# Layer 1's x_w product in halves of a chunk on two column tiles, its step sizes over all rows, and its output as 128 and twice 64 channels

## The chip, the core and the metric

The kernel runs on one core of one Trainium2 chip. The time is the device time of one execution in microseconds (us). The core has TensorE (PE, the matrix engine; PEld is its loading of weights), VectorE (DVE), ScalarE (ACT), GpSimd (POOL) and SyncE (SP, which here only issues DMAs). They run their own instruction streams and wait for each other by semaphores. All data are float32.

## The reference

Four layers work on an image batch of 4 x 64 x 64 positions and 192 channels, each as x + layer(group norm of x). The change is in layer 1, where four selective scans (forward and backward along rows, forward and backward along columns) run on 384 inner channels with 16 states each. For one direction, with `xs` a set of lines of 64 positions:

```python
xz = jnp.einsum('nlc,dc->nld', xs, in_w)
u, z = jnp.split(xz, 2, axis=-1)
uc = silu(conv(u, cw) + cb)                  # 4 taps along the line
x_dbl = jnp.einsum('nld,ed->nle', uc, xw)    # 12 + 16 + 16 rows
dt, Bp, Cp = jnp.split(x_dbl, [DT_RANK, DT_RANK + DS], axis=-1)
delta = jax.nn.softplus(jnp.einsum('nlr,dr->nld', dt, dtw) + dtb)
# step: h = exp(delta * A) * h + delta * uc * B;  y = sum over the states of h * C
y = (y + uc * Dv) * silu(z)
out = jnp.einsum('nld,cd->nlc', y, ow)
```

The results of the four directions are joined and multiplied with `fc_w`. Layers 0 and 3 are two-dimensional selective scans with the same inner loop and layer 2 is a Toeplitz mixing; the change leaves their arithmetic alone.

## The kernel before

Channels lie on the partitions. Layer 1 (`mamba`, L678) first multiplies `fc_w` into the four output matrices, and then makes 128 jobs: 4 directions x 4 images x 8 chunks of T = 512 positions. Directions 1 and 3 are backward and add to what the direction before them has put in DRAM (`done`, written as `m_out`).

**One job.** `mamba_job` (L752) loads the chunk (`xn`, L771), multiplies with `in_w` in three blocks of 128 channels (`input_of`, in_ps, L777), convolves on DVE (L794) and applies silu on ACT. `prepare` (L189) makes the small products: `project` (L196) is x_w's product, 44 x 512 (xd_ps, L211); ACT copies it to `xd` and sends its B and C rows to DRAM (L221); `turn_b` (L232) transposes B; `step_size` (L246) makes the step sizes of one block of 128 channels out of the 12 rows 32 to 43 of `xd` (dt_ps, L261); `finish` applies softplus and forms dtu = delta * u; `turn` transposes dtu. `gate` multiplies with the other half of `in_w` (z_ps). `out` (L817) multiplies with the output matrix, in two pieces of 96 channels (o_ps, L821), and stores to `m_out` (L829); in a backward direction `earlier` (L814) has loaded the values to add.

`project` and `step_size` have a second form, used where `halves` is true, which in this kernel is layer 0 alone: the chunk is split in two halves of 256 positions, whose products stand on partitions 0 to 63 and 64 to 127.

**The units.** The scan itself goes in 24 units a job, each 64 channels with two pairs of states, 128 x 1024 elements. For a unit, `feed` (L340) has TensorE make b = delta * u * B in PSUM by 8 matmuls (L360) and ACT make dA = exp(delta * A) (L383); `scan` has DVE run the recurrence (L393) and POOL multiply by C (hc, L405); `collect` has TensorE sum over the states (y, L423). In 6 of the 24 units (those of one state pair) b is made by POOL (`spread`, bs, L337) in place of TensorE; in a job they are units 2, 5, 10, 13, 18 and 21, counted from 0. b's PSUM pool has two buffers, so the b of a unit waits for the scan two units before.

**The loads.** `fetch` (L295) brings the operands from DRAM to SBUF by SP: C (c) and, for POOL's b, B (bc), each row broadcast over 64 partitions (L325), and the channel rows delta (both) and dtu, each twice, by a source with a leading dimension of 2 (L312). The pools have 4 buffers for c, 4 for both and 2 each for bc and dtu, so a load waits in SP's queue until the unit that used the buffer is done.

**The order.** `run_jobs` (L104) walks all units and puts each job's steps at a number of units before or after the job's first unit: chunk load at -48, `input_of` at -45, -32 and -29, `project` -24, `turn_b` -22, `step_size` -20, -18 and -17, `out` at 32 and 35. The steps of one job so fall among the units of the two jobs before it. A scheduler then settles the order on each engine from estimated times; the engines keep to it.

Of the kernel before, what the change touches and what calls it, by code (L numbers as in the profile page):

```python
# [7 lines left out]
F32 = mybir.dt.float32  # L8
AF = mybir.ActivationFunctionType
# [4 lines left out]
B, HW, L = 4, 64, 4096  # L14
C = 192
PC, KC = 96, 2
N = 16
R = 12
E = R + 2 * N
T = 512  # L20
# [16 lines left out]
class Kernel:  # L37
# [151 lines left out]
    def prepare(self, job, pools):  # L189

        nc = self.nc
        prep, mm = pools["prep"], pools["mm"]
        P, NT, DI, w = job["P"], job["NT"], job["DI"], job["w"]
        halves = job["carry"] is not None and NT == 3

        def project():  # L196
            u = job["u"]
            if halves:

                ps = mm.tile([128, 256], F32, name="xd_ps", tag="mm")  # L200
                for t in range(NT):
                    for h in range(2):
                        nc.tensor.matmul(
                            ps[h * 64 : (h + 1) * 64, :], w["xw"][:, t, :], u[:, t, h * 256 : (h + 1) * 256],
                            start=t == 0, stop=t == NT - 1,
                        )
                xd = job["xd"] = prep.tile([128, 256], F32, name="xd", bufs=1)
            else:
                ps = mm.tile([E, T], F32, name="xd_ps", tag="mm")
                for t in range(NT):  # L210
                    nc.tensor.matmul(ps, w["xw"][:, t, 0:E], u[:, t], start=t == 0, stop=t == NT - 1)  # L211
                xd = job["xd"] = prep.tile([E, T], F32, name="xd", bufs=1)
            nc.scalar.copy(xd, ps)
            job["bc"] = self.bcd.tile([2 * N, T], F32, name="bc_dram")
            if job["carry"] is None:

                by_half = job["bc"].rearrange("(a n) l -> a (n l)", n=2).rearrange(
                    "a (h n l) -> h a n l", h=2, n=2
                )
                for h in range(2):  # L220
                    nc.scalar.dma_start(by_half[h], xd[0 : 2 * N, h * 256 : (h + 1) * 256])  # L221
            elif halves:
                by_half = job["bc"].rearrange("a (h l) -> h a l", h=2)
                for h in range(2):
                    nc.scalar.dma_start(by_half[h], xd[h * 64 : h * 64 + 2 * N, :])
            else:
                nc.scalar.dma_start(job["bc"], xd[0 : 2 * N, :])
            job["delta"] = prep.tile([P, NT, T], F32, name="delta", bufs=1)
            job["dtu"] = prep.tile([P, NT, T], F32, name="dtu", bufs=1)
            job["dtuT"] = prep.tile([128, NB, DI], F32, name="dtuT",)  # L230

        def turn_b():  # L232
            bt = job["bt"] = prep.tile([128, NB, N], F32, name="bt")
            if halves:
                ps = mm.tile([128, 2, 128], F32, name="b_ps", tag="mm")
                for k in range(2):
                    nc.tensor.transpose(ps[:, k, :], job["xd"][:, k * 128 : (k + 1) * 128], self.ident)
                of = ps.rearrange("p k (h e) -> p k h e", h=2)[:, :, :, 0:N]
                nc.scalar.copy(bt.rearrange("p (h k) n -> p k h n", h=2), of)
                return  # L240
            ps = mm.tile([128, NB, N], F32, name="b_ps", tag="mm")
            for k in range(NB):
                nc.tensor.transpose(ps[:, k, :], job["xd"][0:N, k * 128 : (k + 1) * 128], self.ident[:N, :N])
            nc.scalar.copy(bt, ps)

        def step_size(t):  # L246
            if halves:

# [12 lines left out]
            nc.tensor.matmul(  # L261
                dp, w["dtw"][2 * N : E, t * P : (t + 1) * P], job["xd"][2 * N : E, :], start=True, stop=True
            )
            nc.scalar.activation(job["delta"][:, t, :], dp, AF.Identity, bias=w["dtb"][:, t : t + 1])

        def finish():
            delta = job["delta"]
            nc.scalar.activation(delta, delta, AF.Softplus)  # L268
            (nc.gpsimd if job["carry"] is None else nc.vector).tensor_mul(job["dtu"], delta, job["u"])  # L269
            if job["carry"] is not None:  # L270
                return
            job["deltas"] = self.bcd.tile([DI, T], F32, name="delta_dram")
            nc.scalar.dma_start(job["deltas"].rearrange("(t p) l -> p t l", p=P), delta)

        def turn(t):
            ps = mm.tile([128, NB, P], F32, name="dtu_ps", tag="mm")
            for k in range(NB):
                nc.tensor.transpose(  # L278
                    ps[:, k, :], job["dtu"][:, t, k * 128 : (k + 1) * 128], self.ident[:P, :P]
                )  # L280
            nc.scalar.copy(job["dtuT"][:, :, t * P : (t + 1) * P], ps)  # L281

        def store_dtu():
            job["dtus"] = self.bcd.tile([DI, T], F32, name="dtu_dram")
# [393 lines left out]
    def mamba(self, x_in):  # L678
# [3 lines left out]
        DI = P * NT  # L682
        pre = "L1_"
        by_row, by_col = self.image_tiles("m_row"), self.image_tiles("m_col")
        done = [self.image_tiles(f"m_out{i}_") for i in range(2)]

        both_w = [self.dram.tile([P, NT, C], F32, name=f"m_both_w{i}") for i in range(4)]
        bufs = dict(c=4, bc=2, diag=4, both=4, dtu2=2)
# [63 lines left out]
    def mamba_job(self, pw, pin, mm, i, begin, rev, w, x, done, both_w, c, fixed, zero):  # L752
# [6 lines left out]
        job = {}  # L759

        def weights():
            for name in ("in_w", "conv_w", "conv_b", "A", "D", "x_w", "dt_b"):
                w[name] = self.load(pw, name, ins[pre + name][i])
            w["dtw"] = pw.tile([E, DI], F32, name="dt_w")
            nc.sync.dma_start(w["dtw"][2 * N : E, :], ins[pre + "dt_w"][i])
            w["out_w"] = self.load(pw, "out_w", both_w)
            w["xw"], w["dtb"] = w["x_w"], w["dt_b"]
            self.neg_exp(w["A"])

        def load():  # L770
            job["xn"] = self.load(pin, "xn", x[:, :, s])  # L771
# [37 lines left out]
        def gated(t):  # L809
            u, z = job["u"][:, t, :], job["z"][:, t, :]  # L810
            nc.vector.scalar_tensor_tensor(u, u, w["D"][:, t : t + 1], job["y"][t], ALU.mult, ALU.add)
            nc.gpsimd.tensor_mul(z, z, u)

        def earlier(m):  # L814
            job.setdefault("o", {})[m] = self.load(pin, "o", done[:, m, s])

        def out(m):  # L817
            o = job["o"][m] if rev else pin.tile([PC, T], F32, name="o")
            ps = mm.tile([PC, T], F32, name="o_ps", tag="mm")
            for t in range(NT):  # L820
                nc.tensor.matmul(  # L821
                    ps, w["out_w"][:, t, m * PC : (m + 1) * PC], job["z"][:, t, :],
                    start=t == 0, stop=t == NT - 1,
                )
            if rev:
                nc.vector.tensor_add(o, ps, o)
            else:
                nc.scalar.copy(o, ps)
            nc.sync.dma_start(done[:, m, s], o)  # L829

        when = dict(project=-24, turn_b=-22, step_size=(-20, -18, -17), finish=-15, turn=(-10, -7, -3), store=-11)
        each = lambda f, ats: [(at, lambda t=t: f(t)) for t, at in enumerate(ats)]
        steps = [(-50, weights)] if begin else []
        steps += [(-48, load)] + each(input_of, (-45, -32, -29)) + each(gate, (-6, -4, -2)) + each(out, (32, 35))
        if rev:
            steps += each(earlier, (26, 29))
# [8 lines left out]
    def toeplitz(self, x_in, parts, x_out):  # L845
# [7 lines left out]
        with (  # L853
# [5 lines left out]
            for b in range(B):  # L859
                x = pn.tile([PC, KC, L], F32, name="x")  # L860
                rows, cols = (pn.tile([PC, KC, L], F32, name="part") for _ in range(2))
                for k in range(KC):
                    for to, of in ((x, x_in[b]), (rows, parts[b][0]), (cols, parts[b][1])):
                        nc.sync.dma_start(to[:, k, :], of[:, k, :])
# [288 lines left out]
```

## Time and profile before

| | |
|---|---|
| median of 3 runs | 31505.68 us (31467.85 to 31518.7) |
| the profiled execution's own time | 31496.9 us |
| its span, from the first to the last instruction | 31495.0 us |
| mean granted TensorE clock | 0.946 |
| layer 1: first in_ps to last o_ps | 10743.6 to 22109.9 us |
| within layer 1, 12000 to 20000 us: busy share of PE, DVE, ACT, POOL | 95%, 71%, 82%, 87% |
| there, mean busy share of the 16 DMA engines | 31% |
| there, PE waited for xn's DMA | 217 us in 90 waits |
| there, SP waited for POOL's bs before a load of dtu or both | 2348 us in 434 waits |

The profile times every instruction of one execution. A line such as `L360 PE MATMUL b<-diag,dtuT` names the line of the kernel, the engine, the operation and what it writes and reads; one float32 matmul of the program is two instructions, a transpose one. The chain of waits follows the work back from its end: at each step to whatever released it last. What is beside the chain could take longer, up to a point, without moving the end.

### The profile page before, as it was taken

Reading aid. Unit: us, or ns where it says so; the run is one execution under the profiler, and the core shown is the slowest. Engines: PE = TensorE matmul, PEld = TensorE weight load, DVE = VectorE, ACT = ScalarE, POOL = GpSimd, SP = SyncE. Lnnn points to the kernel's source line nnn. Section 1 sums busy time; section 2 is a strip of 40 time slices with the busy share of each in tenths; the row PEclk is TensorE's granted clock in tenths of the full one; section 3 lists DMA queues with packets and bytes.
Section 4 is the critical chain, followed back from the end, with each engine's and each line's share of the span. In section 5 each row is a group of like instructions: output and inputs, shape, how many; then the busy total and the mean of one; then the engine's idle time right before and its main releaser. Section 6 shows DMA issues by size and latency. Waiting matters only on the chain.

```text
span 31495.0 us, 452842 instructions
## 1 busy us (share of the span) xinstructions
PE 28016.1 (89%) x164120; PEld 13777.8 (44%) x164120; DVE 22496.5 (71%) x16587; ACT 23230.4 (74%) x50559; POOL 22921.2 (73%) x9863
## 2 busy tenths in 40 slices
PE   8998998998899699999999999999588988888888
PEld 4554554554455344444444444444355343434344
DVE  7887887888788677777777777777433267677767
ACT  7885885887688488888888888888123187878788
POOL 7885885887688488888888888888000086867777
PEclk9999998999999899999999999999789999999999
DMA  3333333334333433233332333333533454444444
GB/s 105 101 100 114 103 99 115 100 98 112 102 102 100 134 94 93 93 98 98 98 99 92 94 94 96 98 99 98 133 73 71 109 133 121 129 126 127 124 127 125
DMA packets 1586996, 3327.52 MB, mean 106 GB/s; under 512 B 354981, under 2 KB 374166, under 8 KB 1569142
## 3 DMA queue, kind: packets, MB, share of 16 engines
q1 hardware_dynamic: 1418870, 3021.63, 35.1%
q10 hardware_dynamic: 165888, 276.91, 2.6%
q8 instruction: 1299, 21.28, 0.3%
q14 instruction: 939, 7.69, 0.1%
HBM read 2138.38 MB, written 656.08 MB: 89 GB/s over the span
## 4 chain that ended last, share of the span: by engine, by line
PE 39%; DVE 14%; POOL 14%; ACT 13%; DMA 10%; issue 7%; SPq 2%; ACTq 0%; DVEq 0%; POOLq 0%
PE b L360 16%; POOL hc L405 11%; DVE h L400 8%; PE y L423 8%; ACT diag L318 5%; ACT dA L383 4%; DVE h L393 3%; DMA xn<-m_col 3%; DMA xn<-m_row 2%; PE in_ps L777 2%; POOL bs L337 2%; SPq L325 2%; PE yt_ps L1014 2%; PE conv_ps L509 2%; DMA xn<-t_xn 2%
## 5 line engine op out<-in xcount | busy, mean ns | idle before, releaser
L405 POOL TENSOR_TENSOR hc<-h,c 128x1024 f32<-128x1024 f32 x7680 | 18176.9, 2384 | 3019.2 <-DVE h L393 1288.0
L360 PE MATMUL b<-diag,dtuT 128*64 128x256 f32 x98304 | 12662.5, 392 | 955.3 <-DVE h L400 829.9
L360 PEld LDWEIGHTS b<-diag,dtuT 128*64 128x64 f32 x98304 | 7451.4, 140 | 6835.4 <-issue 3023.8
L400 DVE TENSOR_TENSOR_SCAN h<-dA,carry,b 128x512 f32<-128x512 f32 x6720 | 8187.4, 1264 | 1696.7 <-PE b L360 875.4
L423 PE MATMUL y<-hc,fold 128*64 128x512 f32 x30720 | 8832.2, 601 | 579.8 <-POOL hc L405 566.2
L383 ACT ACTIVATE dA<-both,A 128x512 f32<-128x512 f32 (+1 forms) x12288 | 8306.5, 711 | 305.7 <-DVE h L393 181.0
L393 DVE TENSOR_TENSOR_SCAN h<-dA,b 128x1024 f32<-128x1024 f32 x2304 | 5251.9, 2284 | 2064.3 <-PE b L360 900.9
L318 ACT ACTIVATE diag<-ident,bt 128x128 f32<-128x128 f32 x20480 | 6514.8, 391 | 123.5 <-ACT b L383 83.2
L337 POOL TENSOR_TENSOR bs<-dtu,bc 128x1024 f32<-128x1024 f32 x1536 | 3639.0, 2369 | 300.0 <-DMA dtu<-dtu 172.2
L423 PEld LDWEIGHTS y<-hc,fold 128*64 128x64 f32 x30720 | 2462.3, 138 | 2969.2 <-POOL hc L405 1263.2
L477 POOL MEMSET pad<- 128x13068 f32 (+1 forms) x8 | 73.5, 9187 | 3972.7 <-DMA cw<-in_L_conv_w 3005.2
L383 ACT ACTIVATE b<-both,A 128x504 f32<-128x504 f32 (+1 forms) x3072 | 2077.4, 676 | 283.0 <-DVE h L400 237.0
L393 DVE TENSOR_TENSOR_SCAN h<-b,bs 128x1024 f32<-128x1024 f32 x768 | 1754.3, 2284 | 658.6 <-ACT b L383 387.6
L403 ACT COPY carry<-h 128x2 f32<-128x2 f32 x4608 | 849.6, 184 | 1233.8 <-DVE h L400 1015.3
L400 DVE TENSOR_TENSOR_SCAN h<-b,carry,bs 128x512 f32<-128x512 f32 x1344 | 1638.2, 1259 | 105.5 <-POOL hc L405 94.2
L400 DVE TENSOR_TENSOR_SCAN h<-dA,b 128x512 f32<-128x512 f32 x960 | 1112.4, 1205 | 425.3 <-ACT dA L383 165.4
L383 ACT ACT_TABLE_LOAD x1018 | 1306.1, 1283 | 16.8 <-ACT b L371 0.3
L777 PE MATMUL in_ps<-xn,in_w 96*128 96x512 f32 x1536 | 943.6, 746 | 333.4 <-DMA xn<-m_row 173.3
L794 DVE SCALAR_TENSOR_TENSOR u<-in_ps,conv_w,u 128x504 f32<-128x504 f32 (+2 forms) x1152 | 835.8, 725 | 475.3 <-ACT u L789 454.0
L269 DVE TENSOR_TENSOR dtu<-delta,u 128x1536 f32<-128x1536 f32 (+1 forms) x256 | 607.4, 2373 | 541.6 <-ACT delta L268 541.6
L278 PEld LDWEIGHTS dtu_ps<-ident,dtu 128*128 128x128 f32 (+1 forms) x4096 | 421.5, 142 | 874.2 <-issue 554.0
L777 PE MATMUL z_ps<-xn,in_w 96*128 96x512 f32 x1536 | 761.7, 618 | 0.3 <-ACT dtuT L281 0.2
(163 smaller groups left out, 21940.7 us busy)
## 6 DMA issues: line engine op xcount, KB each, us to landing
c<-bc_dram SPq DMA_DIRECT2D x3072, 256.0 KB
both<-delta SPq DMA_DIRECT2D x2048, 128.0 KB
bc<-bc_dram SPq DMA_DIRECT2D x768, 256.0 KB
both<-delta_dram SPq DMA_DIRECT2D x768, 256.0 KB
dtu<-dtu_dram SPq DMA_DIRECT2D x768, 256.0 KB
dtu<-dtu SPq DMA_DIRECT2D x1280, 128.0 KB
L_y<-out ACTq DMA_DIRECT2D x512, 256.0 KB
u<-L_u SPq DMA_DIRECT2D x160, 768.0 KB
```

Of the source, the lines that this page charges most:

```text
L318: nc.scalar.activation(to, self.ident, AF.Copy, scale=of)
L325: nc.sync.dma_start(one[q * 64 : (q + 1) * 64, :], src.unsqueeze(0).broadcast_to([64, 2 * T]))
L337: self.nc.gpsimd.tensor_mul(by(b), dtu, by(job["bbc"][p]))
L360: nc.tensor.matmul(to, job["dtuT"][:, k, g * 64 : (g + 1) * 64], job["diag"][p][:, k, 2 * q : 2 * q + 2, :], start=True, stop=True,)
L383: nc.scalar.activation(to[n], of, AF.Exp, scale=w["A"][:, g, 2 * p + n : 2 * p + n + 1])
L393: nc.vector.tensor_tensor_scan(h[:, way], dA[:, way], b[:, way], 0.0, ALU.mult, ALU.add)
L400: nc.vector.tensor_tensor_scan(hn[:, n, way], dA[:, n, way], by_n[:, n, way], start, ALU.mult, ALU.add)
L403: nc.scalar.copy(carry[g, p], hn[:, :, 0 if rev else T - 1])
L405: nc.gpsimd.tensor_mul(hc, h, job["cbc"][p])
L423: nc.tensor.matmul(y[c * 64 : (c + 1) * 64, :], self.fold, of, start=first == 0 and n == 0, stop=last == LAST and n == 1)
L777: nc.tensor.matmul(ps, w["in_w"][:, k, to + t * P : to + (t + 1) * P], job["xn"][:, k, :], start=k == 0, stop=k == KC - 1,)
L794: nc.vector.scalar_tensor_tensor(u[:, :, to], ps[:, :, of], tap(3 - j), u[:, :, to], ALU.mult, ALU.add)
```

## The change

`halves` becomes true for layer 1 too, and `split` keeps layer 0's way of making the step sizes for layer 0. In layer 1:

- x_w's product is made as 2 x 64 rows x 256 positions: for each of three blocks, one matmul for either half of the chunk, on either half of TensorE's columns. x_w is padded with zeros to 64 columns (`xw`). `xd` is 128 x 256.
- `turn_b` makes two full transposes in place of four small ones.
- `step_size` uses all 128 rows of `xd` and, for each half, a matrix `dtw` that is zero except in that half's 12 rows. It is cleared and loaded at the start of each direction (`weights_of_steps`, at -40, one buffer).
- `out` makes channels 0 to 127 as one product, and channels 128 to 191 as two halves of the chunk on two column tiles. Stores and `earlier` loads go in three DMAs in place of two, with two buffers for the first piece and one for the second. `m_out` is laid out as 192 rows.
- layer 2 reads `m_out` by the same 96 rows as before, from the new layout.

```diff
-        halves = job["carry"] is not None and NT == 3
+        halves, split = NT == 3, job["carry"] is not None
...
         def step_size(t):
+            if halves and not split:
+                dp = mm.tile([P, T], F32, name="dt_ps", tag="mm")
+                for h in range(2):
+                    nc.tensor.matmul(
+                        dp[:, h * 256 : (h + 1) * 256], w["dtw"][:, h, t * P : (t + 1) * P], job["xd"],
+                        start=True, stop=True,
+                    )
+                nc.scalar.activation(job["delta"][:, t, :], dp, AF.Identity, bias=w["dtb"][:, t : t + 1])
+                return
...
-            w["dtw"] = pw.tile([E, DI], F32, name="dt_w")
-            nc.sync.dma_start(w["dtw"][2 * N : E, :], ins[pre + "dt_w"][i])
+            w["xw"] = pw.tile([P, NT, 64], F32, name="xw")
+            nc.gpsimd.memset(w["xw"][:, :, E:64], 0.0)
+            nc.sync.dma_start(w["xw"][:, :, 0:E], ins[pre + "x_w"][i])
...
+        def weights_of_steps():
+            w["dtw"] = pw.tile([128, 2, DI], F32, name="dt_w", bufs=1)
+            nc.gpsimd.memset(w["dtw"], 0.0)
+            for h in range(2):
+                nc.sync.dma_start(w["dtw"][h * 64 + 2 * N : h * 64 + E, h, :], ins[pre + "dt_w"][i])
...
+        half = T // 2
+        pieces = [[(slice(0, 128), done[0:128, s])], [
+            (slice(h * 64, (h + 1) * 64), done[128:C, c * T + h * half : c * T + (h + 1) * half]) for h in range(2)
+        ]]
...
         def earlier(m):
-            job.setdefault("o", {})[m] = self.load(pin, "o", done[:, m, s])
+            o = job.setdefault("o", {})[m] = pin.tile([128, (T, half)[m]], F32, name=f"o{m}", bufs=2 - m)
+            for rows, of in pieces[m]:
+                nc.sync.dma_start(o[rows], of)
 
         def out(m):
-            o = job["o"][m] if rev else pin.tile([PC, T], F32, name="o")
-            ps = mm.tile([PC, T], F32, name="o_ps", tag="mm")
+            o = job["o"][m] if rev else pin.tile([128, (T, half)[m]], F32, name=f"o{m}", bufs=2 - m)
+            ps = mm.tile([128, (T, half)[m]], F32, name="o_ps", tag="mm")
             for t in range(NT):
-                nc.tensor.matmul(
-                    ps, w["out_w"][:, t, m * PC : (m + 1) * PC], job["z"][:, t, :],
-                    start=t == 0, stop=t == NT - 1,
-                )
+                z = job["z"][:, t, :]
+                if m == 0:
+                    nc.tensor.matmul(ps, w["out_w"][:, t, 0:128], z, start=t == 0, stop=t == NT - 1)
+                for h in range(2 * m):
+                    nc.tensor.matmul(
+                        ps[h * 64 : (h + 1) * 64], w["out_w"][:, t, 128:C], z[:, h * half : (h + 1) * half],
+                        start=t == 0, stop=t == NT - 1,
+                    )
...
-            nc.sync.dma_start(done[:, m, s], o)
+            for rows, to in pieces[m]:
+                nc.sync.dma_start(to, o[rows])
...
-        steps = [(-50, weights)] if begin else []
+        steps = [(-50, weights), (-40, weights_of_steps)] if begin else []
```

More of the change, by code (lines that the diff above doesn't have):

```diff
@@ L219, in project @@
                 )
-                for h in range(2):
-                    nc.scalar.dma_start(by_half[h], xd[0 : 2 * N, h * 256 : (h + 1) * 256])
-            elif halves:
+            else:
                 by_half = job["bc"].rearrange("a (h l) -> h a l", h=2)
+            if halves:
                 for h in range(2):
@@ L684, in mamba @@
         by_row, by_col = self.image_tiles("m_row"), self.image_tiles("m_col")
-        done = [self.image_tiles(f"m_out{i}_") for i in range(2)]
+        done = [[self.dram.tile([C, L], F32, name=f"m_out{i}_{b}") for b in range(B)] for i in range(2)]
         both_w = [self.dram.tile([P, NT, C], F32, name=f"m_both_w{i}") for i in range(4)]
@@ L761, in weights @@
         def weights():
-            for name in ("in_w", "conv_w", "conv_b", "A", "D", "x_w", "dt_b"):
+            for name in ("in_w", "conv_w", "conv_b", "A", "D", "dt_b"):
                 w[name] = self.load(pw, name, ins[pre + name][i])
-            w["dtw"] = pw.tile([E, DI], F32, name="dt_w")
-            nc.sync.dma_start(w["dtw"][2 * N : E, :], ins[pre + "dt_w"][i])
+            w["xw"] = pw.tile([P, NT, 64], F32, name="xw")
+            nc.gpsimd.memset(w["xw"][:, :, E:64], 0.0)
+            nc.sync.dma_start(w["xw"][:, :, 0:E], ins[pre + "x_w"][i])
             w["out_w"] = self.load(pw, "out_w", both_w)
-            w["xw"], w["dtb"] = w["x_w"], w["dt_b"]
+            w["dtb"] = w["dt_b"]
             self.neg_exp(w["A"])
+        def weights_of_steps():
[3 more added lines that the diff above has]
+                nc.sync.dma_start(w["dtw"][h * 64 + 2 * N : h * 64 + E, h, :], ins[pre + "dt_w"][i])
         def load():
@@ L862, in toeplitz @@
                 for k in range(KC):
-                    for to, of in ((x, x_in[b]), (rows, parts[b][0]), (cols, parts[b][1])):
-                        nc.sync.dma_start(to[:, k, :], of[:, k, :])
+                    nc.sync.dma_start(x[:, k, :], x_in[b][:, k, :])
+                    for to, of in zip((rows, cols), parts[b]):
+                        nc.sync.dma_start(to[:, k, :], of[k * PC : (k + 1) * PC, :])
                 for k in range(KC):
```

## The prediction

> **What bounds the kernel now.** I read the page first (TensorE is the busiest engine), then layer 1 alone: the chain of waits through one chunk, the timelines of PE and POOL, and the DMA view.
>
> ```profile
> PE 28016.1 (89%) x164120; PEld 13777.8 (44%) x164120; DVE 22496.5 (71%) x16587; ACT 23230.4 (74%) x50559; POOL 22921.2 (73%) x9863
> ```
>
> TensorE alone would suggest that every matmul saved is time saved. The chain of waits in 15000 to 15190 us (start, length, what) says otherwise:
>
> ```profile
> 15079.18 3.78 PE in_ps L777 x4
> 15082.97 2.77 PE b L360 x16
> ...
> 15094.02 1.90 PE b L360 x16
> ...
> 15096.04 2.30 DVE h L393
> ...
> 15098.47 2.09 POOL hc L405
> ...
> 15103.15 2.33 POOL bs L337
> ...
> 15154.81 12.82 DMA xn<-m_row
> ...
> 15167.68 3.78 PE in_ps L777 x4
> ```
>
> One turn is one chunk, 88.5 us (15167.68 - 15079.18). Neither the product with x_w (L211) nor an output product (L821) is on it, only two of the three step sizes (L261). A turn has two parts. From in_ps to the end of that bs (15105.5) the engines set the pace: 26.3 us. From there to the next in_ps it is DMA: 62.2 us, where TensorE waits at the end for xn. The following chunks show the same split: bs ends 15194.1, 15282.8, 15371.6 (starts 15191.74, 15280.47, 15369.20, each 2.36); next in_ps 15256.41, 15345.12, 15433.93; so 62.3, 62.3, 62.3. Why it is fixed, the DMA view of 15095 to 15109 shows, 40 slices of 0.35 us: busy tenths of 16 engines, then GB/s.
>
> ```profile
> DMA  1111111111111111110000599999400002683111
> GB/s 53 47 53 47 53 53 47 53 47 53 53 47 53 47 53 53 47 41 23 23 0 0 193 386 380 380 374 380 152 0 0 0 0 12 176 275 123 12 47 47
> ```
>
> A load of both or dtu runs at about 50 GB/s with a tenth of the engines busy. Page part 6 gives 768 loads of each from DRAM over 128 chunks, so 12 a chunk of 256 KB: 12 x 5.3 us (262 KB at 49 GB/s) = 64 us, and c, bc, xn and the stores pass the same engines. The zeros are the only idle time of a turn: the queue waits there for the bs that frees dtu's buffer (15105.5). Then all that follows in SP's order, xn last, drains without a pause. TensorE and POOL just before in_ps (start, length, ..., idle before):
>
> ```profile
> 15064.78 2.74 PE L211 MATMUL xd_ps<-u,x_w 128*44 128x512 f32 x6
> ...
> 15071.63 2.13 PE L360 MATMUL b<-diag,dtuT 128*64 128x256 f32 x16
> ...
> 15079.18 3.78 PE L777 MATMUL in_ps<-xn,in_w 96*128 96x512 f32 x4 [3.40 <-DMA xn<-m_row]
> ```
> ```profile
> 15077.57 6.98 POOL L405 TENSOR_TENSOR hc<-h,c 128x1024 f32<-128x1024 f32 x3
> 15084.49 2.38 POOL L337 TENSOR_TENSOR bs<-dtu,bc 128x1024 f32<-128x1024 f32 x1
> 15088.25 2.38 POOL L405 TENSOR_TENSOR hc<-h,c 128x1024 f32<-128x1024 f32 x1 [1.38 <-DVE h L393]
> ```
>
> The second b (unit 4 of the chunk) runs ahead of the wait for xn; so units 4 and 5 are scanned, and their two hc and a bs are with POOL, while xn is awaited.
>
> **What the Trainium skill says.** "DMA: Bandwidth & Descriptors", section "Rules for kernel authors": an outermost dimension smaller than 16, such as a leading broadcast, confines a DMA to that many engines. L312 reads with a leading 2: two of 16, which agrees with the tenths of 1 and 50 GB/s. "TensorE: Matmul & The Clock Gate", "Part 3: Packing small matmuls": matmuls keep program order and different column tiles run together. Layer 0 has the new form of x_w already: 12 instructions in 1.47 us (10017.12), so it agrees. Its "Part 1": an idle TensorE falls to half clock and comes back only after sustained work. Agrees: after 3.40 us idle in_ps takes 3.72 us to the next b, against 1.91 elsewhere, and the b after it 2.77 against 1.73.
>
> **The change part by part.** I compared the order of instructions in the two built programs, which a scheduler sets, for each chunk of layer 1.
>
> *x_w's product.* 2.74 becomes 1.47 us (layer 0's row): 1.27 less for TensorE. It lies ahead of the wait for xn, so the wait grows by 1.27. The copy of xd goes from 0.575 to 0.35 us on ACT, equally covered. bc is stored about 1.5 us earlier, but bc's loads stand behind xn in SP's queue.
>
> *Transposes.* 4 of 16 columns (0.42 us) become 2 of 128 (two in 0.44 at 168.87): nothing, and ahead of the same wait.
>
> *Step sizes.* 2 passes of 512 columns become 4 of 256, on 128 rows: the same 1024 columns; 1.05 us before. No row shows the new form; from 0.85 (nothing for switching) to 1.4 (four uncovered loads of weights, 4 x 0.19, on part of it). I take 1.05, so 0.
>
> *Outputs.* First one: M from 96 to 128, same columns, 2.74. Second: 12 passes of 256 on two tiles, 1.47 by the x_w row, 1.3 less. Both are at 15009 and 15018, beside POOL's unbroken hc and bs; not on the chain: 0. SP issues three stores instead of two, and three loads where the direction is reversed, at 0.46 us each (m_out at 15016.72); SP sat 2348 us in 8000 waiting for bs, which covers them. Bytes are equal.
>
> *Starts of a direction.* Clearing dt_w (128x768, beside 0.97 us for 128x1024 of L807), xw's tail, and a wait for the last step size, which holds SP's loads behind it: four times; between 0 and 10 us each. I take 0, as 15.8 us were waited there already.
>
> *Order.* ACT gets 126 more table loads in layer 1 by the built program (1.28 us each): one a chunk, in the DMA-bound part: 0, at worst 1.3. And TensorE's order round in_ps:
>
> ```
> before: x_w product, b3, y x3, b4, y, transposes, y x2, in_ps (both halves), b6, ...
> after:  x_w product, y x3, b3, y, transposes, y x2, in_ps (first half), b4, in_ps (second half), y, b6, ...
> ```
>
> In 118 of 127 chunks b4 now stands behind the first matmul that waits for xn. That is a stall added, and its queue is all of units 4 and 5. Worked from in_ps's start as zero, by the rows above: first half of in_ps 1.86 at the low clock; b4 3.4 (twice 1.73), to 5.3; scan 4 (2.29) to 7.7. DVE's next three are the convolution's (0.73 each; their input is there at 7.1) to 9.9; scan 5 (2.29) to 12.2. Now POOL has hc5, bs10, hc6 to hc10 and bs13 in a row, none of which can start earlier: 8 x 2.35 = 18.8, to 31.1. Its inputs keep up: by the same sums scan 9 ends at 22.0 and is wanted at 24.1. Before, this bs ended at 26.3. So a turn grows by 4.8 us; the DMA part, which starts with that bs, keeps its 62. Over some 125 turns: +600 us. Against the profiled run (span 31495.0, run 31496.9) that is 32097, and the median of the runs lies 9 us above it: 32105, say 32100.
>
> What is uncertain: if the low clock were gone, b4 ends 2.5 us sooner: +2.3 a turn, +290. If it lasts longer (the idle time grows from 3.4 to some 6.5 us) and the table load falls on the path, +7 a turn, +880. Step sizes, two on the chain: -0.4 to +0.7 a turn, -50 to +90.
>
> **Rivals.** *TensorE is the bound after all*, as its 95% within layer 1 suggests: 2.6 us less in each of 128 chunks, 31497 - 333 = 31160. Against it: the saved products are not on the chain, and xn is waited for in nearly every chunk (90 times in 8000 us). It is the case on the other side. It needs DMA to have over 2.6 us of slack a turn; the zeros above show about that much, but after the bs, not before xn. *Nothing changes*: b4's delay is caught up by DVE and POOL before bs13, and the savings stay hidden: 31500. For it: POOL idles 1.4 + 1.5 + 0.2 + 1.5 us between bs10 and hc9; against: the delay is larger. *Only TensorE is late*, by one b and a switch (+2.0) while POOL catches up: +2.0 x 125 = 250, 31750. For it POOL would have to do eight pieces in less than 18.8 us.
>
> **How the numbers follow.** Bs13 late by 4 to 7 us a turn: 0.68. Only TensorE late: 0.17. Nothing: 0.06. Faster: 0.09. The range from 31720 to 32400 holds the first two but for their edges, 0.8. This kernel's measurement tells 0.2% (63 us) from no change; so faster 0.09, same 0.06, slower 0.85.
>
> **What would show it.** In the chain, b right behind half an in_ps, then POOL hc and bs without idle time up to bs13 at about +31 us; a turn of 93 us; the zeros of the DMA view grown from about 2 us (6 slices of 0.35) to 7; PE's wait for xn grown to 6 us or more; xd_ps at 1.47 and o_ps at 2.8 and 1.5 us. Wrong it is if turns stay at 88 us or shrink, if bs13 comes at +26, or if the DMA part is no longer 62 us.

## The result and the profile after

The changed kernel takes 32030.4 us (median of 4 runs, 32008.9 to 32064.0) against 31512.2 us of the kernel before, measured with it: a ratio of 1.0169, 95% interval 1.0157 to 1.0181. The profiled execution has a span of 32033.8 us, 538.8 more than before, at the same mean clock (0.946). The chain of waits of this profile doesn't reach back into layer 1, so the timelines are read instead.

The page of the changed kernel, part 1 (busy time, share of the span, instructions):

```profile
PE 28089.5 (88%) x166168; PEld 14099.5 (44%) x166168; DVE 22428.5 (70%) x16587; ACT 23380.9 (73%) x50685; POOL 22909.6 (72%) x9871
```

PE is busy 73 us longer than before and ACT 151, PEld 322 beside the matmuls, and DVE and POOL less, so most of the 539 us is waiting time. Within 12000 to 20000 us PE is busy 7254 us, where it was 7576, and POOL 6634 against 6989: the same engines with more idle time. The new forms cost what the prediction took. The timeline of PE round 15071 to 15116 us of the changed kernel (start, length, line, output <- inputs, count; consecutive equal instructions are one row):

```profile
15071.23 1.47 PE L204 MATMUL xd_ps<-u,xw 128*64 128x256 f32 x12
...
15100.68 1.13 PE L250 MATMUL dt_ps<-xd,dt_w 128*128 128x256 f32 x4
...
15106.55 2.84 PE L849 MATMUL o_ps<-z,out_w 128*128 128x512 f32 x6
...
15115.40 1.47 PE L851 MATMUL o_ps<-z,out_w 128*64 128x256 f32 x12
```

The x_w product went from 2.74 to 1.47 us and the second output from 2.8 to 1.47. A group of step sizes takes 1.07 us to the start of the next instruction (15101.75, from the same view), 1.05 before.

Where the time went is seen at in_ps. The same view, at a chunk of direction 2:

```profile
17300.48 1.08 PE L432 MATMUL y<-hc,fold 128*64 128x512 f32 x4
17305.89 1.38 PE L795 MATMUL in_ps<-xn,in_w 96*128 96x512 f32 x2 [4.34 <-DMA xn<-m_col]
17307.20 3.30 PE L369 MATMUL b<-diag,dtuT 128*64 128x256 f32 x16
17310.44 1.13 PE L795 MATMUL in_ps<-xn,in_w 96*128 96x512 f32 x2
```

The brackets give the idle time ahead of a row and what ended it. Unit 4's b (17307.20) waits with in_ps for xn, between its halves. What hangs on it, in the timelines of DVE and POOL:

```profile
17310.65 2.29 DVE L402 TENSOR_TENSOR_SCAN h<-dA,b 128x1024 f32<-128x1024 f32 x1 [8.82 <-PE b L369]
```
```profile
17313.02 2.39 POOL L414 TENSOR_TENSOR hc<-h,c 128x1024 f32<-128x1024 f32 x1 [5.83 <-DVE h L402]
17317.45 2.37 POOL L414 TENSOR_TENSOR hc<-h,c 128x1024 f32<-128x1024 f32 x1 [2.04 <-DVE h L402]
17319.77 2.37 POOL L346 TENSOR_TENSOR bs<-dtu,bc 128x1024 f32<-128x1024 f32 x1
17322.10 11.65 POOL L414 TENSOR_TENSOR hc<-h,c 128x1024 f32<-128x1024 f32 x5
17333.68 2.39 POOL L346 TENSOR_TENSOR bs<-dtu,bc 128x1024 f32<-128x1024 f32 x1
```

DVE idles 8.82 us for b4, and POOL 5.83 for DVE. From hc5 (17317.45) POOL works without a pause through hc5, bs10, five hc and bs13, which ends at 17336.07: 30.2 us after in_ps's start. Only then does SP get its buffer back. DVE's waits for b over 12000 to 20000 us sum this up (waiting line <- what ended the wait: us, times, longest), before and after:

```profile
DVE h L393 <- PE b L360: 633.2, 709, 3.0
```
```profile
DVE h L402 <- PE b L369: 1037.2, 370, 14.5
```

Half as many waits, longer in sum by 404 us, and the longest is 14.5 us where none was above 3.0.

The DMA view of 17328 to 17342 us, 40 slices of 0.35 us:

```profile
DMA  1111111111000008999990000007841111159999
GB/s 53 47 53 47 47 53 47 53 47 47 23 0 0 0 0 339 392 404 380 386 334 12 0 0 0 0 12 193 345 158 53 47 53 53 47 222 392 386 404 380
```

Eight slices with no byte moved (2.8 us), where the view of before has six: SP's queue waits for bs13 as before, and somewhat longer. The burst between the empty slices is ScalarE's store of delta, which stands in the view of before too. Over whole turns (123 of each trace, pauses of over 0.1 us) DMA is idle for 4.5 us a turn, where it was 2.4.

The directions are not alike. PE's waits at in_ps for xn in directions 0, 1, 2 and 3 (windows inside each, of 2650, 2600, 2500 and 2200 us; us in sum, times, longest), one answer for each:

```profile
PE in_ps L795 <- DMA xn<-m_row: 115.5, 28, 6.2
```
```profile
PE in_ps L795 <- DMA xn<-m_row: 19.3, 16, 2.9
```
```profile
PE in_ps L795 <- DMA xn<-m_col: 130.0, 27, 6.0
```
```profile
PE in_ps L795 <- DMA xn<-m_col: 15.0, 11, 6.0
```

The kernel before had 65 to 74 us in each of these. So in the forward directions (0 and 2) the wait is 1.7 and 2 times as long, and in the backward ones (1 and 3) it has nearly gone: something else is late there.

A table of the turn, as means over 123 chunks of each trace, with in_ps's start as zero. The last three columns are where b4 and bs13 end, and what passes from bs13's end to the next in_ps ("the DMA part"). The experiments' rows are read below. Where input_of is moved (-44, -46, -47), in_ps itself stands elsewhere in the order, so there the turn is compared rather than the two ends. The ratios given with the experiments are to the kernel before as measured with each run (31492.7 to 31512.2 us).

| kernel | median us | turn | b4 ends | bs13 ends | DMA part |
|---|---|---|---|---|---|
| before | 31512 | 88.32 | -4.47 | 26.23 | 62.09 |
| after | 32030 | 92.47 | 3.83 | 29.49 | 62.99 |
| 1 after, b4 first | 31650 | 89.44 | -4.01 | 26.20 | 63.24 |
| 2 after, in -44 | 31654 | 89.28 | -2.00 | 24.64 | 64.64 |
| 3 after, in -46 | 32257 | 94.32 | 5.68 | 31.27 | 63.04 |
| 4 outputs only | 31505 | 88.22 | -4.46 | 26.04 | 62.18 |
| 5 x_w and step sizes only | 31588 | 89.10 | -4.02 | 26.04 | 63.06 |
| 6 before, wide loads | 31040 | 84.72 | -1.95 | 25.14 | 59.58 |
| 7 after, wide loads | 31522 | 88.61 | 2.84 | 28.40 | 60.21 |
| 8 b4 first, wide loads | 30988 | 84.33 | -0.18 | 24.94 | 59.39 |
| 9 before, in -47 | 32069 | 92.80 | 6.56 | 30.73 | 62.08 |
| 10 in -46, gates earlier | 32335 | 94.89 | 6.09 | 31.69 | 63.20 |
| 11 in -44, gates earlier | 31379 | 87.31 | -4.09 | 23.39 | 63.92 |
| 12 as 11, wide loads | 31272 | 86.62 | -3.45 | 23.33 | 63.29 |

A turn has grown by 4.15 us, 3.26 of it up to bs13's end and 0.90 behind it; over 128 chunks that is 531 of the 539 us.

And by pairs of directions, where "b4" is its end counted from the end of the scan of unit 1:

| kernel | turn, directions 0 and 2 | b4 | turn, directions 1 and 3 | b4 |
|---|---|---|---|---|
| before | 88.39 | 5.44 | 88.24 | 5.44 |
| after | 92.64 | 13.99 | 92.30 | 10.66 |
| 1 after, b4 first | 88.86 | 6.79 | 90.03 | 6.82 |
| 2 after, in -44 | 87.54 | 7.53 | 91.06 | 8.82 |
| 6 before, wide loads | 84.69 | 5.44 | 84.75 | 5.44 |
| 7 after, wide loads | 86.25 | 7.91 | 91.01 | 9.21 |
| 8 b4 first, wide loads | 84.24 | 6.77 | 84.41 | 6.81 |

### The profile page after: what moved, and what is told of

The parts are those of the page before. It is cut to its first block, busy times and chain, and to the rows that moved or that the text cites. A ratio compares the mean times of both kernels' runs of the same rounds, so it can differ in the third digit from the quotient of the medians.

```text
span 32033.8 us, 456906 instructions
## 1 busy us (share of the span) xinstructions
PE 28089.5 (88%) x166168; PEld 14099.5 (44%) x166168; DVE 22428.5 (70%) x16587; ACT 23380.9 (73%) x50685; POOL 22909.6 (72%) x9871
## 5 line engine op out<-in xcount | busy, mean ns | idle before, releaser
L369 PE MATMUL b<-diag,dtuT 128*64 128x256 f32 x98304 | 12918.4, 393 | 1108.2 <-DVE h L409 832.5
L369 PEld LDWEIGHTS b<-diag,dtuT 128*64 128x64 f32 x98304 | 7639.5, 140 | 6660.1 <-issue 2936.6
L432 PE MATMUL y<-hc,fold 128*64 128x512 f32 x30720 | 9490.6, 604 | 856.4 <-POOL hc L414 856.2
L432 PEld LDWEIGHTS y<-hc,fold 128*64 128x64 f32 x30720 | 2563.5, 138 | 3595.7 <-POOL hc L414 1735.3
L807 ACT ACTIVATE u<-in_ps,conv_w 128x512 f32<-128x512 f32 x384 | 262.3, 683 | 1288.4 <-PE in_ps L795 1276.6
L795 PE MATMUL in_ps<-xn,in_w 96*128 96x512 f32 x1536 | 855.7, 669 | 349.5 <-DMA xn<-m_row 171.8
```

The costliest lines, as they stand in the source:

```text
L369: nc.tensor.matmul(to, job["dtuT"][:, k, g * 64 : (g + 1) * 64], job["diag"][p][:, k, 2 * q : 2 * q + 2, :], start=True, stop=True,)
L432: nc.tensor.matmul(y[c * 64 : (c + 1) * 64, :], self.fold, of, start=first == 0 and n == 0, stop=last == LAST and n == 1)
L795: nc.tensor.matmul(ps, w["in_w"][:, k, to + t * P : to + (t + 1) * P], job["xn"][:, k, :], start=k == 0, stop=k == KC - 1,)
```

## The experiments

The theory: the scheduler's order puts b4 behind half of in_ps, and everything to bs13 is late by that. The rivals: (A) x_w's and the step sizes' new matmuls cost by themselves; (B) the outputs' new layout and smaller transfers; (C) ScalarE's 126 added table loads.

### 1. The changed kernel with b4 ahead of in_ps

```diff
-                nc.tensor.matmul(
+                self.last_b = nc.tensor.matmul(
                     to, job["dtuT"][:, k, g * 64 : (g + 1) * 64], job["diag"][p][:, k, 2 * q : 2 * q + 2, :],
                     start=True, stop=True,
-                )
+                ).ins
...
+            with ExitStack() as order:
+                if name == "in" and t == 0 and getattr(self, "last_b", None) is not None:
+                    order.enter_context(self.tc.issue_after(self.last_b))
```

> The changed kernel with one ordering edge more: TensorE's matmuls of a chunk's first in_ps are issued behind the b matmuls of the unit traced just before them, so that b4 stands ahead of both halves of in_ps, as it does before the change. Nothing else of the change is undone; the 126 added table loads of ScalarE are gone with it as well. Theory (b4 behind the wait for xn costs 3.3 us a chunk, measured on the end of bs13): bs13 ends 26.0 to 26.8 us after in_ps's start, against 29.5, and the whole takes 31510 to 31640 us (32030 less 3.3 x 125; the 0.9 us that the DMA part has grown may stay or go). Rival A, the change's own matmuls (x_w by halves on column tiles, step sizes on all rows) are what costs: it stays within 80 us of 32030. Rival B, the new layout of the output and its smaller transfers are what costs: it also stays within 80 us of 32030. Rival C, the 126 added table loads: at most 161 us go, so not below 31870.

Measured: 31649.8 us, ratio to before 1.0045 (1.0030 to 1.0060). One edge of order takes back 381 of the 518 us; bs13 ends at 26.20 us, as before the change. In a chunk of direction 2, PE and POOL:

```profile
17086.70 1.67 PE L369 MATMUL b<-diag,dtuT 128*64 128x256 f32 x13
...
17090.40 1.96 PE L799 MATMUL in_ps<-xn,in_w 96*128 96x512 f32 x4 [1.33 <-DMA xn<-m_col]
```
```profile
17090.19 4.68 POOL L414 TENSOR_TENSOR hc<-h,c 128x1024 f32<-128x1024 f32 x2
17096.26 2.36 POOL L414 TENSOR_TENSOR hc<-h,c 128x1024 f32<-128x1024 f32 x1 [1.39 <-DVE h L402]
17098.58 2.37 POOL L346 TENSOR_TENSOR bs<-dtu,bc 128x1024 f32<-128x1024 f32 x1
17100.91 11.70 POOL L414 TENSOR_TENSOR hc<-h,c 128x1024 f32<-128x1024 f32 x5
17112.56 2.38 POOL L346 TENSOR_TENSOR bs<-dtu,bc 128x1024 f32<-128x1024 f32 x1
```

b is done when xn comes, POOL has two hc to do meanwhile and idles 1.39 us where it idled 5.83. A and B fall as the main cause. The time is slightly above the upper end expected: the DMA part stays at 63.24, 1.15 us over before. C can't be told apart here, as the added loads went too.

### 2 and 3. input_of one unit later and one earlier

```diff
-each(input_of, (-45, -32, -29))
+each(input_of, (-44, -32, -29))     # run 2
+each(input_of, (-46, -32, -29))     # run 3
```

> The changed kernel with input_of(0) due one unit later (-44 for -45). TensorE's order then has two b units between xd_ps and in_ps, as before the change, with b4 ahead of in_ps, and the unit after the next (b6) between its halves; ScalarE's 126 added table loads stay. Theory (only a b unit that POOL needs next is dear behind the wait): the 3.3 us mostly go: 31500 to 31750 us; b4 ends before in_ps starts. Rival C (the table loads are what costs): it stays near 32030, not below 31950. Rival D (any b between the halves costs the same): 31950 to 32050.

> The changed kernel with input_of(0) due one unit earlier (-46 for -45). TensorE's order then has both halves of in_ps ahead of b4, and only one b unit between xd_ps and in_ps. Theory: b4 waits for the same xn and for one half more (1.0 us): bs13 ends 30 to 31.5 us after in_ps's start, and the whole takes 32000 to 32200 us. Rival (it is the splitting of in_ps by a b unit, with its switch in and out of the tiling, that costs): 31500 to 31700.

Measured: 31654.1 us (1.0044; 1.0029 to 1.0059) and 32257.4 us (1.0237; 1.0222 to 1.0252). Both keep all of the change's operations and the added table loads. The place of the same two matmuls moves the whole by 603 us. At -46 it is dearer than expected by 57 us over the range's end. At -44 another b (unit 6's) stands between the halves, and it does not cost what b4's does: rival D falls. C falls as the cause of most of the 518 us, since the loads are still there. But the directions differ: a turn takes 87.85 and 87.25 us in directions 0 and 2, 91.18 and 90.93 in 1 and 3. Run 11 takes this up.

### 4 and 5. Each half of the change alone

Run 4 keeps the diff of `out`, `earlier`, `m_out` and layer 2's load; the 44-row x_w and the two-pass step sizes are those of before. Run 5 keeps `halves`, `split`, `project`, `turn_b`, `step_size` and their weights, with the outputs of before:

```diff
-        halves = job["carry"] is not None and NT == 3
+        halves = split = NT == 3 and job["carry"] is not None     # run 4
+        halves, split = NT == 3, job["carry"] is not None         # run 5
...
-        done = [self.image_tiles(f"m_out{i}_") for i in range(2)]
+        done = [[self.dram.tile([C, L], F32, name=f"m_out{i}_{b}") for b in range(B)] for i in range(2)]     # run 4
```

> Only the change's output part: o as 128 channels and as twice 64 channels of half a chunk, m_out as [C, L], its loads and stores in three pieces a chunk; x_w's product and the step sizes as before the change (the weights of the step sizes in one buffer, loaded at -40). TensorE's order around in_ps is that of before. Theory: TensorE saves 1.3 us a chunk that nothing waits for, so 31440 to 31570 us, the same as before. Rival B (the new layout and its smaller transfers cost on SyncE's queue or on the DMA engines): over 31650, up to 32030.

> Only the change's x_w and step size parts (x_w by halves of a chunk on two column tiles, its copy of 128 rows, the step sizes over all 128 rows with two matmuls per piece); output and m_out as before. TensorE's order has b4 ahead of in_ps without any edge added, and ScalarE has no added table loads. Theory (with b4 ahead, what is left of the loss is the part from the end of bs13 to the next in_ps, 63.2 us in the run with b4 first against 62.1 before, and 62.2 with the output part alone, so it comes with x_w and the step sizes): 31600 to 31690 us, that part 62.9 to 63.4 us. Rival (the remainder needs both parts together, or comes of the edge added): 31470 to 31550. Rival A (x_w and the step sizes cost by themselves on TensorE, whatever the order): over 31750.

Measured: 31505.0 us (0.9999; 0.9990 to 1.0007) and 31587.6 us (1.0025; 1.0017 to 1.0034). In both, TensorE's order has b4 ahead of in_ps with no edge added, so neither half alone brings the loss: it takes both for the scheduler's estimates to tip b4 over. The 1.3 us that the outputs save are worth nothing (B falls), and those of x_w are outweighed. Run 5 is 12 us under the range expected: its loss is 80 us. What x_w and the step sizes cost by themselves is in the DMA part (63.06 against 62.09). From the trace, SP issues xn 49.65 us after bs13's end there, 49.01 before, and from the issue to in_ps it is 13.40 and 13.07: so two thirds of it is that xn is issued later, by 0.33 us in directions 0 and 2 and 0.95 in 1 and 3. Nearly all of that is one instruction, the issue of a load of c two places ahead of xn in SP's queue: it starts 44.2 us after bs13's end in both kernels, and takes 4.08 us for 3.84 in directions 0 and 2, and 4.97 for 4.05 in 1 and 3. Why it takes longer was not tried.

### 6, 7 and 8. The two-engine loads

```diff
-                nc.sync.dma_start(one, src.unsqueeze(0).broadcast_to([2, 64, T]))
+                for q in range(2):
+                    nc.sync.dma_start(one[q * 64 : (q + 1) * 64, :], src)
```

in the kernel before (6), in the changed kernel (7), and in run 1's kernel (8).

> The kernel before with one edit: each both and dtu load of layer 1 (L312, one DMA of 128 rows whose source repeats 64 rows twice) as two DMAs of 64 rows. Theory (the part from bs13 to the next in_ps is set by these loads, each carried by 2 of the 16 DMA engines at some 50 GB/s, 12 a chunk): they spread over 16 engines, that part falls from 62.1 us to what TensorE needs, a chunk takes 84 to 86 us (TensorE is busy 95% of 88.3), and the whole 30950 to 31300 us. Rival (the loads are hidden, POOL or TensorE sets that part): 31440 to 31600.

> The changed kernel with the same edit of the both and dtu loads. Theory (the wait for xn that b4 stands behind is itself a wait behind those loads on SyncE's queue): xn comes early, b4 is no longer late, and the change's shorter TensorE work counts: a chunk takes 82.5 to 85 us, 30700 to 31200 us, no slower than the kernel before with that edit. Rival (xn comes as late as ever): as much slower than the kernel before with that edit as the change is without it, some 400 to 540 us. Rival (the loads are hidden): 31950 to 32100.

> Both: the changed kernel with b4 issued ahead of in_ps and with the both and dtu loads as two DMAs of 64 rows. Theory: with xn early the order hardly matters, so within 100 us of the changed kernel with the wide loads, 30650 to 31200 us. Rival (xn still late): 300 us or more below it. Rival (the loads are hidden): 31570 to 31720.

Measured: 31039.9 us (0.9848; 0.9833 to 0.9862), 31521.7 us (1.0002; 0.9994 to 1.0011) and 30987.7 us (0.9831; 0.9816 to 0.9846). Run 8 is the fastest kernel found, faster than both kernels of the case; its four runs (30983.0 to 30991.1) lie wholly under those of run 6 (31036.1 to 31043.6).

Run 6's DMA view of 17028 to 17042 us, again in slices of 0.35 us around the end of bs13 (17039.8):

```profile
DMA  7000000000000000000000003999996000000655
GB/s 228 29 0 0 0 0 0 0 0 0 0 0 0 0 0 0 0 0 0 0 0 0 0 0 135 392 380 398 369 363 217 0 0 12 12 18 0 193 182 82
```

The long rows of 47 to 53 GB/s are gone: DMA idles where it moved bytes without a pause. The burst is again ScalarE's store of delta. The loads themselves are seen in the view of 17016 to 17030 us: eight of the halves (1.05 MB) move in 15 slices, at 200 GB/s.

```profile
DMA  0000076777587995895200000000000167620000
GB/s 0 0 0 0 0 164 234 123 228 240 187 228 199 222 269 164 293 275 117 76 0 0 0 0 0 0 0 0 0 0 0 47 222 182 193 105 0 0 0 0
```

So the DMA part was bound by these loads, as predicted, and the Trainium skill's rule on an outermost dimension under 16 ("DMA: Bandwidth & Descriptors", "Rules for kernel authors") agrees. Another limit stands close behind: with DMA idle for 43 us of a turn, the part is only 2.5 us shorter. TensorE is busy 97% of 12000 to 20000 us there; whether it is that limit was not tried.

Run 7 is the surprise. Its time is what the rival "xn comes as late as ever" gave, 482 us above run 6, but not for that reason: among PE's waits over 12000 to 20000 us, in_ps has none for xn at all (275 us in the changed kernel). The pairs of directions tell more. In 0 and 2, b4 ends at 7.91 where run 8 has 6.77: without the wait for xn the order alone makes it 1.1 us late, and the turn is 2.0 us longer. In 1 and 3 the turn is 91.01 us, 6.6 longer than in run 8. There DVE stands elsewhere, in unit 21, half a turn away from in_ps. DVE in run 7, direction 1:

```profile
13819.10 2.28 DVE L403 TENSOR_TENSOR_SCAN h<-dA,b 128x1024 f32<-128x1024 f32 x1
13826.81 2.29 DVE L403 TENSOR_TENSOR_SCAN h<-b,bs 128x1024 f32<-128x1024 f32 x1 [5.43 <-ACT b L393]
```

It waits 5.43 us for ACT's exp. This is where the added table loads stand; run 7 has them and runs 6 and 8 have not. Run 2 has them too, and its turn there is 91.06 with the narrow loads: so a turn takes 91.0 us with these loads whether xn comes early (run 7) or b4 does (run 2). So "with xn early the order hardly matters" was wrong because the order on ScalarE matters as well: 534 us lie between runs 7 and 8, some 128 (64 x 2.0) in the forward and some 420 (64 x 6.6) in the backward directions.

### 9. b4 behind in_ps without the change

```diff
-each(input_of, (-45, -32, -29))
+each(input_of, (-47, -32, -29))     # the kernel before
```

> The kernel before with nothing of the change, only input_of(0) due two units earlier (-47 for -45). TensorE's order then has both halves of in_ps ahead of b4, and is as before elsewhere; no table load is added. Theory (b4 behind in_ps is what costs, and none of the change's own operations is needed for it): b4 ends 4 to 7 us after in_ps's start, bs13 30 to 32 us after it (26.2 before), and the whole takes 31950 to 32300 us. Rival (the place of b4 is dear only together with the change's x_w, step sizes or outputs): 31440 to 31650.

Measured: 32069.2 us, 1.0182 (1.0167 to 1.0197). PE, and POOL behind it:

```profile
17343.99 3.75 PE L777 MATMUL in_ps<-xn,in_w 96*128 96x512 f32 x4 [6.65 <-DMA xn<-m_col]
17347.67 3.34 PE L360 MATMUL b<-diag,dtuT 128*64 128x256 f32 x16
```
```profile
17353.56 2.38 POOL L405 TENSOR_TENSOR hc<-h,c 128x1024 f32<-128x1024 f32 x1 [7.54 <-DVE h L393]
17356.38 2.36 POOL L405 TENSOR_TENSOR hc<-h,c 128x1024 f32<-128x1024 f32 x1 [0.44 <-PE y L423]
17358.70 2.38 POOL L337 TENSOR_TENSOR bs<-dtu,bc 128x1024 f32<-128x1024 f32 x1
17361.04 11.80 POOL L405 TENSOR_TENSOR hc<-h,c 128x1024 f32<-128x1024 f32 x5
```

This is the pattern of the changed kernel, with none of the change's operations and no added table load, and the loss is as large (576 us). The turn grows by 4.48 us, all of it up to bs13 (26.23 to 30.73); the DMA part stays at 62.08. That b4's place suffices is shown by this run. That it is what costs in the changed kernel is shown by run 1 for directions 0 and 2, where no table load was added; in 1 and 3 run 1 took the loads away too.

### 10, 11 and 12. The added table loads

The gates of two tiles one unit earlier take the 126 loads away and leave TensorE's order at in_ps as it is:

```diff
-each(gate, (-6, -4, -2))
+each(gate, (-7, -5, -2))
```

with input_of at -46 (10) and -44 (11), and with the wide loads besides (12).

> The changed kernel with input_of(0) at -46, as in the run before of that kind (32257 us), and the gates of its first two tiles due one unit earlier (-7, -5, -2): TensorE's order around in_ps is that of the -46 run, but ScalarE's 126 added table loads are gone. Theory (where b4 is late the loads lie beside the wait for xn): 32150 to 32290 us. Rival (each added load is on the path, two a chunk in two of the four directions): 161 us or more less, 31950 to 32100.

> The changed kernel with input_of(0) at -44, as in the run before of that kind (31654 us), and the gates due one unit earlier (-7, -5, -2): b4 is ahead of in_ps as in that run, and ScalarE's 126 added table loads are gone. There a chunk took 87.5 us in directions 0 and 2 and 91.0 in 1 and 3, where the added loads are. Theory (with b4 early, the added loads and what stands behind them on ScalarE are what is left of the loss): directions 1 and 3 fall to 87.5 to 88.6 us, 31430 to 31520 us, no slower than the kernel before. Rival (the loads are hidden, the directions differ for another reason): 31600 to 31700.

> The run with b4 early and the gates one unit earlier, and the both and dtu loads as two DMAs of 64 rows. Theory (neither b4, nor the table loads, nor the two DMA engines are late, TensorE's shorter work decides): a chunk takes 83.5 to 84.5 us, 30850 to 31000 us, 40 to 190 us less than the kernel before with the same loads (31040). Rival (POOL's chain of scans sets the chunk, not TensorE): 31000 to 31100, the same as that.

Measured: 32335.2 us (1.0267; 1.0252 to 1.0282), 31378.8 us (0.9963; 0.9950 to 0.9976) and 31272.1 us (0.9928; 0.9912 to 0.9945).

With b4 late at -46, taking the loads away gains nothing (run 10 is 78 us above run 3, 45 outside the range). In directions 1 and 3 DVE's mean wait in unit 21 falls from 5.31 to 0.89 us there, but PE's for xn at in_ps grows from 1.95 to 7.07 and DVE's for b4 from 6.15 to 10.33: the time that the loads took is waited for xn instead. With b4 early it gains 275 us (2 to 11; run 11 is 51 us under the range expected): in directions 1 and 3 a turn falls from 91.06 to 86.76 us, in 0 and 2 it goes from 87.54 to 87.85. The loads are in directions 1 and 3 only: 14 a chunk in place of 12, by the trace of run 2. ACT in run 2, and the wait of DVE that ends with it:

```profile
13889.96 1.28 ACT L815 ACT_TABLE_LOAD   x1
13891.25 0.72 ACT L815 ACTIVATE u<-u,conv_b 128x512 f32<-128x512 f32 x1
13891.99 1.28 ACT L392 ACT_TABLE_LOAD   x1
13893.29 0.69 ACT L392 ACTIVATE b<-both,A 128x504 f32<-128x504 f32 x1
13893.99 1.28 ACT L820 ACT_TABLE_LOAD   x1
13895.28 0.60 ACT L820 ACTIVATE z<-z_ps 128x512 f32<-128x512 f32 x1
13895.90 1.28 ACT L392 ACT_TABLE_LOAD   x1
13897.19 0.68 ACT L392 ACTIVATE b<-both,A 128x504 f32<-128x504 f32 x1
```
```profile
13897.98 2.29 DVE L402 TENSOR_TENSOR_SCAN h<-b,bs 128x1024 f32<-128x1024 f32 x1 [5.43 <-ACT b L392]
```

Silu of u, exp, silu of z, exp: four switches of table in a row, and the second exp is what DVE waits for, as in run 7. The same wait stands in the changed kernel, and was shorter before it (a chunk of direction 1 of each):

```profile
14596.38 2.29 DVE L402 TENSOR_TENSOR_SCAN h<-b,bs 128x1024 f32<-128x1024 f32 x1 [5.43 <-ACT b L392]
```
```profile
14430.32 2.29 DVE L393 TENSOR_TENSOR_SCAN h<-b,bs 128x1024 f32<-128x1024 f32 x1 [2.10 <-ACT b L383]
```

On average it is 5.31 us for 2.10 in directions 1 and 3, and 2.19 for 2.10 in 0 and 2. In run 11 u and z go together behind one load, and DVE's wait at that place is 0.89 us. Moving the gates moves the z products too, so the 4.3 us a turn are those of the loads and of that place together.

Run 11 is the change with three due times moved, and is 0.37% faster than the kernel before. Run 12 missed its range by 272 us: with that order the wide loads bring 107 us, not the 380 or more expected. Counted from unit 13, the scans of units 14 to 26 come on average at the same times in runs 11 and 12, within 0.03 us, and 1.0 to 3.1 us later than in run 8. So in that stretch neither the loads nor DMA set the pace in run 12; what in the new order does was not tried.

## Why the prediction was right, and where it was off

**The mechanism.** "In 118 of 127 chunks b4 now stands behind the first matmul that waits for xn" (in the trace it is 119 of 126): run 9 (the order alone) and, in directions 0 and 2, run 1 (the order undone) show from both sides that this place costs what was lost. The direction, the forecast of 32100 us and the range were right; the time was 70 us less. But the reason holds as it was given in half of the chunks only. In directions 0 and 2, b4 waits for xn and the turn grows by 4.25 us; with b4 early 3.8 (run 1) to 5.1 (run 2) of it go. In directions 1 and 3 the turn grows by nearly the same 4.06, and there two things are late, b4 and the table loads. With b4 early and the loads kept (run 2) 1.2 us go, with both gone (run 1) 2.3.

**The sum, term by term.** "First half of in_ps 1.86 at the low clock; b4 3.4 ..., to 5.3" was too long: b4 ends at 3.83 on average. The low clock was taken for every chunk; in the trace the second instruction of in_ps runs at it in 57 of 123 chunks (97 before), 51 of them in directions 0 and 2. In the chunk shown above the clock falls within that instruction: the half takes 1.38 us, b4 behind it 3.30, and b4 ends 4.6 us after in_ps's start. From b4's end to bs13's the prediction had 25.8 us (5.3 to 31.1); measured 25.66, and from hc5 to bs13 18.62 in the chunk shown, for 18.8. So bs13 came 1.6 us earlier than predicted, 29.49 for 31.1, nearly all of it from the first term.

**"The DMA part ... keeps its 62."** It became 62.99. That xn is issued later on SP's queue was not seen; run 5 shows that x_w's and the step sizes' part brings this by itself (63.06). The two errors, -1.6 and +0.9, offset each other in part: 4.15 us a turn for 4.8.

**Costed at nothing.** The outputs: right (run 4). x_w's 1.27 us: right that they are hidden, but that half of the change isn't free (80 us in run 5). Table loads, "one a chunk, in the DMA-bound part: 0, at worst 1.3": wrong in count, place and size. They are two a chunk in the backward directions, DVE waits for them, and a turn there takes 91.1 us with them and b4 ahead of in_ps (run 2), 2.8 more than before, and 86.8 without them (run 11). b4 is late in the same turns and the two overlap, so the total came out right with this step wrong: for directions 1 and 3 that was luck. The changed kernel with its b4 late and without the loads was not run; run 10 is the nearest to it.

**The rivals.** "Nothing changes" and "only TensorE is late" assumed that POOL catches up. It does not: its 18.6 us from hc5 to bs13 are unbroken. "TensorE is the bound after all" was rightly put aside for this kernel. With the loads spread, the 2.6 us a chunk saved on TensorE are worth 0.4 (84.72 to 84.33), so even there it isn't TensorE alone.

**The signs.** b behind half an in_ps, POOL unbroken to bs13, xd_ps and o_ps at their new lengths: seen. The idle slices of the DMA view were to grow to 7 us, and are 2.8 in the turn shown; all pauses of a turn, also those ahead of that view, make 4.5 (run 9: 6.3). PE's wait for xn was to be 6 us; it is 4.1 and 4.8 on average in directions 0 and 2 (115.5 / 28 and 130.0 / 27).

**Open.** Why the issue of c ahead of xn takes SP longer, above all in directions 1 and 3, and with it the 140 us that run 1 keeps over the kernel before.

## What to carry to other kernels

A saving on an engine that isn't on the chain is worth nothing, but shorter operations change a scheduler's order, and the order can cost more than the operations do: compare the built order around every instruction that waits for a transfer, and around every switch of ScalarE's table, and ask what another engine wants soon that now queues there. A due time moved by one unit is a cheap trial: here it was worth 376 us (-45 to -44). Look at each kind of iteration by itself, since the turns of forward and backward directions grew alike (4.25 and 4.06 us) for different reasons.

## What the runs showed of the hardware that was not expected

- A load of 128 rows from a source with a leading 2 ran at 47 to 53 GB/s. As two DMAs of 64 rows each, such loads moved at 200 GB/s (1.05 MB in 15 slices of 0.35 us, run 6). It is twice the DMAs issued, and the kernel is 1.5% faster.
- TensorE's low clock at in_ps comes with the wait ahead of it and goes with it. In run 9, with 7.0 us of idle time ahead of in_ps (601 us in 86 waits), in_ps runs at it in 123 of 123 chunks (3.75 us, and 3.34 for the b behind it, where 1.98 and 1.95 are usual); in runs 6 and 7, where nothing waits for xn, in none. In run 7 it stands elsewhere: in 47 chunks unit 3's b, behind 2.3 to 2.4 us of waiting for DVE, takes 3.2 to 3.7 us. The Trainium skill ("TensorE: Matmul & The Clock Gate", "Part 1") says the same of idle time, but names a window of about 3.4 us; here the shorter pause was enough.
- A switch of ScalarE's table took 1.28 us and nothing besides (run 2): 0.02 us from the end of one ACTIVATE to the load, and 0.01 from the load to the next.
